# A conditioned transformer layer: the second norm made tile by tile on VectorE with Newton steps, and its rows of blocks 1 to 13 turned on VectorE through DRAM

## The chip, the core and the metric

The kernel runs on one core of a Trainium2 chip. A core has five engines that run their own instruction queues side by side and meet only at semaphores: TensorE (PE in the profile; PEld are its weight loads), VectorE (DVE), ScalarE (ACT), GpSimd (POOL), and SyncE (SP), which here issues the DMA transfers. Matmul results land in PSUM, everything else on the chip lives in SBUF, and weights and activations come from DRAM. The metric is the device time of one execution in microseconds (us).

## What is computed

The reference is one transformer layer whose two norms are shifted, scaled and gated by a condition. Cut to what matters (8 sequences of 1024 tokens, 512 channels, 16 heads, float32):

```python
mod = silu(condition) @ Wada + bada
sh_a, sc_a, gt_a, sh_m, sc_m, gt_m = split(mod, 6, axis=1)
xn = layernorm(x, g1, be1)
xm = xn * (1.0 + sc_a) + sh_a
x = x + gt_a * attention(xm, Wqkv, Wproj, bproj)     # causal, 16 heads of 32
xn = layernorm(x, g2, be2)                            # the second norm
xm = xn * (1.0 + sc_m) + sh_m
h = gelu(xm @ W1 + b1)
x = x + gt_m * (h @ W2 + b2)
```

`layernorm` subtracts the mean of a row and multiplies by `rsqrt(var + 1e-5)`. The two pairs of vectors around a norm (its own gain and bias, and the shift and scale of the condition) are folded into one gain and one shift for each channel.

## The kernel before

**Blocks and steps.** The 8192 tokens are cut into 16 blocks of 512 (`NB`, two to a sequence), a block into four tiles of 128 rows (`NTT`). A window of the plan (`plan[w]`) holds linear steps: for block w-1 the output projection (`proj`), the second norm's modulated rows (`mt`), the feed-forward's up steps (`u`, four) and down steps (`d`, four); for block w+1 the query and key steps (`k`, `q`); for block w the value step (`v`); and for block w+2 the load, the first norm and its modulated rows (`load_xa`, `norm_a`, `at`). Beside these runs the attention of block w (`attend`): scores into a PSUM region of four banks (`st`), their row maxima on VectorE (line 1556), the exponential on ScalarE (line 1644), the sums of the weights on GpSimd (line 1762). The big linear steps are multiplied with Strassen's seven products (`strassen`), so each takes sums of its operands: `modulated` leaves both the modulated rows (`xm`) and their sums (`t`).

**What sets the order.** The kernel is written by a planner that runs when the program is built. It keeps a modelled clock for each engine (`now`), notes each instruction's modelled length (`note`, `note_pe`, `note_act`), and records next the thread (linear main, linear sides, attention) whose operands are ready first. The recorded order of each engine is then fixed: on the chip an engine works through its own list in that order and waits where an operand is late. `note(..., port=True)` lets a VectorE instruction start after the GpSimd instruction that the model has running at that time. Work that has no fixed place stands in lists (`jobs` for VectorE, `act_jobs`, `pool_jobs`) that are emptied when the model has the engine free. `either` puts an addition on VectorE or GpSimd, `sooner` puts an operation on VectorE or ScalarE, by the modelled clocks. Three PSUM banks (`banks`) serve all linear products, eight SBUF slots (`RING`) the weights, which SP fetches in the order of use as slots come free.

**The second norm before.** `project_out(n)` makes the four tiles of the projection: 16 matmul groups, for each tile the product with the gate row (line 193, VectorE) and the addition to the residual `xr` (`add_to`, VectorE or GpSimd). Behind the last tile `normalize` puts four jobs for VectorE in the list (`bn_stats`, `bn_aggr`, lines 590 and 591); the last of them records `power` on GpSimd (lines 612 to 615: add epsilon, power -1/2, two operations for the offset, on 128x4 each), and four applications of the norm (`apply_tile`) on ScalarE (line 631) or VectorE (line 626) into the tile `hat`, of which there is one buffer. `modulated` then turns the rows into columns on TensorE: 16 matmuls against the identity for a block (line 735), four into a bank, and a modulation of each bank by ScalarE (line 745) or VectorE (line 739). `by_pe` names the norms treated so: all second norms (m0 to m15) and the first norms a0 and a1.

**The first norm of blocks 2 to 15** takes the other way already: the same `normalize`, then `turn`: four stream transposes of 32x32 blocks on VectorE (line 671), a DMA of the 1 MB tile to DRAM (`held`, line 680), four DMAs back into the `hat` tile with the pieces in their places (line 685), and modulations from SBUF. The planner allows 8000 ns (`HOLDING`) for each way.

Of the kernel before, what the change touches and what calls it, by code (L numbers as in the profile page):

```python
# [8 lines left out]

F32 = mybir.dt.float32  # L10
BF16 = mybir.dt.bfloat16
AF = mybir.ActivationFunctionType
ALU = mybir.AluOpType
AX = mybir.AxisListType
# [3 lines left out]
EPS = 1e-5  # L18
# [4 lines left out]
def kernel(  # L23
# [204 lines left out]
    def mlp_steps(n):  # L228
# [62 lines left out]
    def pieces_of(step):  # L291
# [112 lines left out]
    minus_half = const.tile([P, NTT], F32, tag="minus_half", name="minus_half")  # L404
    nc.gpsimd.memset(minus_half, -0.5)
# [171 lines left out]

    hats = {}

    def normalize(tiles, key, sources):  # L580

        for t in range(NTT):
            written["hat", key, t] = NEVER
        mv = small.tile([P, NTT, 2], F32, tag="mv", name=f"mv_{key}")
        rstd = small.tile([P, NTT], F32, tag="rstd", name=f"rstd_{key}")
        offset = small.tile([P, NTT], F32, tag="offset", name=f"offset_{key}")

        def statistics(t):
            st = small.tile([P, nc.vector.BN_STATS_DIM], F32, tag="st", name=f"st_{key}_{t}")
            nc.vector.bn_stats(st, tiles[:, t, :])  # L590
            nc.vector.bn_aggr(mv[:, t, :], st)
# [12 lines left out]
        def root():  # L604
            nc.scalar.activation(rstd, mv[:, :, 1], AF.Sqrt, bias=eps)
            note_act(300, "sqrt", [("mv", key)], [("rstd", key)])
            nc.vector.reciprocal(rstd, rstd)
            nc.vector.scalar_tensor_tensor(offset, mv[:, :, 0], -1.0, rstd, ALU.mult, ALU.mult)
            note("DVE", 360, [("rstd", key)], [("rstd", key)], port=True)

        def power():
            nc.gpsimd.tensor_scalar(rstd, mv[:, :, 1], EPS, None, ALU.add)
            nc.gpsimd.tensor_tensor(rstd, rstd, minus_half, ALU.pow)
            nc.gpsimd.tensor_scalar(offset, mv[:, :, 0], -1.0, None, ALU.mult)
            nc.gpsimd.tensor_tensor(offset, offset, rstd, ALU.mult)
            note("POOL", 1500, [("mv", key)], [("rstd", key)])

        to = [None]

        def apply_tile(t):  # L620
            if t == 0:
                hats[key] = to[0] = hat_tile(key) if key[0] == "m" else tiles
            xh, xt = to[0][:, t, :], tiles[:, t, :]
            reads, writes = [("rstd", key)], [("hat", key, t)]
            if (key == "a0" and t % 2) if alone[0] else sooner(reads, writes, 700, 800) == "DVE":
                nc.vector.tensor_scalar(
                    xh, xt, rstd[:, t : t + 1], offset[:, t : t + 1], ALU.mult, ALU.add
                )
                note("DVE", 700, reads, writes, port=True)
            else:  # L630
                nc.scalar.activation(
                    xh, xt, AF.Identity, bias=offset[:, t : t + 1], scale=rstd[:, t : t + 1]
                )
                note_act(800, None, reads, writes)

        for t in range(NTT):
            add_job(lambda t=t: statistics(t), [sources[t]], key[0] == "m")

    def normalize_tile(xt, key, t, source):

# [22 lines left out]
    def turn(key, rows, xm):  # L663

        small_blocks = xm.rearrange("p c n -> p (c n)")
        by_tile = small_blocks.rearrange("p (m h t i) -> p h m t i", m=NTT, h=NC, t=NTT)
        written["blocks", key] = NEVER

        def turn_tile(t):
            into = by_tile[:, :, :, t, :]  # L670
            nc.vector.transpose(into, rows[:, t, :].rearrange("p (h m i) -> p h m i", m=NTT, i=Q))
# [8 lines left out]
        nc.sync.dma_start(held, small_blocks)  # L680
        written["held", key] = now["PE"] + HOLDING
        yield [("held", key)], []
        for m in range(NTT):
            some = held[:, ts(m, D)].rearrange("(a i) d -> i a d", i=Q)
            nc.sync.dma_start(rows[ts(m, Q), :, :], some)
        written["turned", key] = now["PE"] + HOLDING
        yield [("turned", key)], []
# [4 lines left out]
    def modulated(key, gain, shift, b, guards):  # L692
        for t in ("B11", "B21", "B22", "T1", "T2", "T3", "T4"):
            written[key, t] = NEVER
        turned = key not in by_pe
        if turned:
            yield [*(("hat", key, t) for t in range(NTT)), *guards], []
        else:
            yield [("hat", key, 0), *guards], [BANK]
        got = hats.pop(key)  # L700
# [312 lines left out]
    def project_out(n):  # L1013
# [2 lines left out]
        attT = qTs[n]  # L1016
        tiles = [residual[n][:, t, :] for t in range(NTT)]
        last = n == NB - 1
        begun = []

        def begin(t):
# [6 lines left out]
        for t, xt in enumerate(tiles):  # L1028
# [34 lines left out]
    def up(step):  # L1063
        _, n, q = step
# [217 lines left out]
    def perform(step):  # L1282
# [25 lines left out]
        elif kind == "mt":  # L1308
            n = step[1]
            guards = [("v done", n + 1)]  # L1310
            start(modulated(f"m{n}", *columns_of["m"], blocks[n][0], guards))
        elif kind == "k":
            if step[1] != 3:
# [625 lines left out]
```

## Time and profile before

| | |
|---|---|
| Time, median of 3 runs (lowest to highest) | 3546.16 us (3545.45 to 3546.95) |
| Time of the profiled execution | 3542.2 us |
| Its span, first to last instruction | 3540.5 us |
| Granted TensorE clock, mean | 0.998 |
| Busy: PE, DVE, POOL, ACT | 98%, 61%, 59%, 34% |
| Moved by DMA | 465.96 MB, 132 GB/s on average |

A row of a group gives line, engine, operation, tiles and shapes, the count, then the busy time in us and the mean duration of one in ns, then the idle time of the engine just before them and what ended it. A row of a timeline gives the start and the length in us; neighbours of one kind are merged. Float32 matmuls stand in the trace as two instructions each, and four of them, one for each group of 32 columns or rows, run side by side, so the busy time of a group is far below count times mean. A PE that is busy all the time has no idle time to lose; what it does can still be shortened, and idle time can be added.

### The profile page before, as it was taken

The numbers are of one execution on the slowest core, as the hardware profiler recorded it, in microseconds if no ns is written. First come the engines' busy times: TensorE is split into PE (matmuls) and PEld (weight loads), VectorE is DVE, ScalarE is ACT, GpSimd is POOL, SyncE is SP. The second block draws the span as 40 slices with busy tenths as digits, with TensorE's granted clock in tenths as the row PEclk, the third lists the DMA queues.
The fourth block names the chain that finished last, engine by engine and source line by source line (L and its number), as shares of the span: only waits on it lengthen the run. The fifth ranks groups of instructions, "written<-read, shape, count | busy, mean of one in ns | idle before, by whom it ended". The sixth has DMA issues, their size and how long they took to land.

```text
span 3540.5 us, 120499 instructions
## 1 busy us (share of the span) xinstructions
PE 3482.5 (98%) x54621; PEld 1738.0 (49%) x54621; DVE 2174.2 (61%) x2383; ACT 1190.1 (34%) x1237; POOL 2074.9 (59%) x2249
## 2 busy tenths in 40 slices
PE   8999999999999999999999999999999999999999
PEld 4444445445554555545554454544545445454445
DVE  5776675564756557565675656656566556655563
ACT  2334323352333513235232342323423234232521
POOL 2667836666376664666546675366762667526660
PEclk9999999999999999999999999999999999999999
DMA  6753434335443354524445334443344533443334
GB/s 198 245 163 103 137 117 140 111 111 156 117 148 103 110 160 117 168 85 126 142 118 159 103 115 141 124 149 107 118 132 127 156 106 119 135 126 124 100 110 140
DMA packets 319555, 465.96 MB, mean 132 GB/s; under 512 B 26300, under 2 KB 176636, under 8 KB 316996
## 3 DMA queue, kind: packets, MB, share of 16 engines
q1 hardware_dynamic: 318928, 458.22, 42.9%
q8 instruction: 430, 7.05, 0.8%
q14 instruction: 81, 0.66, 0.1%
q10 hardware_dynamic: 116, 0.03, 0.0%
HBM read 412.99 MB, written 43.06 MB: 129 GB/s over the span
## 4 chain that ended last, share of the span: by engine, by line
PE 88%; DMA 4%; DVE 3%; POOL 2%; issue 1%; ACT 1%; SPq 0%; ACTq 0%; DVEq 0%; POOLq 0%
PE bank L202 61%; PE sc L1541 8%; PE po L1672 7%; PE st L1632 7%; PE st L1620 3%; DMA w<-in_L_cond_Wproj_dram 2%; PE bank L1693 2%; PE bank L735 1%; DVE mx L1556 1%; POOL pT L1762 1%; DMA w<-in_L_cond_Wada_dram 1%; PE bank L1594 0%; POOL hT L161 0%; POOL xr L161 0%; DVE sc L1553 0%
## 5 line engine op out<-in xcount | busy, mean ns | idle before, releaser
L1762 POOL TENSOR_TENSOR pT<-pT,pT 128x256 f32<-128x256 f32 (+3 forms) x1254 | 1207.2, 998 | 347.9 <-PE po L1672 181.4
L1644 ACT ACTIVATE pT<-st 128x2048 f32<-128x2048 f32 x288 | 541.0, 1879 | 1000.5 <-PE st L1632 883.3
L202 PE MATMUL bank<-w,hT 128*32 128x256 f32 x14336 | 812.3, 380 | 1.1 <-ACT rec L1702 0.9
L1556 DVE TENSOR_REDUCE mx<-sc 128x4 f32<-128x2048 f32 (+3 forms) x384 | 666.0, 1755 | 197.7 <-PE sc L1541 191.6
L202 PEld LDWEIGHTS bank<-w,hT 128*32 128x32 f32 x14336 | 450.4, 110 | 369.2 <-issue 81.4
L202 PE MATMUL bank<-xm_m,w 128*32 128x256 f32 x8192 | 499.6, 381 | 0.0
L202 PE MATMUL bank<-t_m,w 128*32 128x256 f32 x6144 | 381.2, 380 | 0.0
L1649 POOL TENSOR_SCALAR_AFFINE_SELECT pT<-pT 128x512 f32<-128x512 f32 x256 | 168.8, 677 | 346.6 <-ACT pT L1644 344.2
L202 PEld LDWEIGHTS bank<-xm_m,w 128*32 128x32 f32 x8192 | 255.7, 110 | 224.7 <-issue 62.4
L1553 DVE TENSOR_TENSOR sc<-sc,mask 128x1024 f32<-128x1024 f32 (+1 forms) x160 | 162.9, 1018 | 319.7 <-PE sc L1541 242.5
L1541 PE MATMUL sc<-kT,qT 32*128 32x512 f32 (+3 forms) x3072 | 329.1, 520 | 1.8 <-DVE mx L1556 1.1
L1672 PE MATMUL po<-pT,v 128*32 128x512 f32 (+3 forms) x3048 | 302.9, 492 | 2.0 <-POOL pT L1649 2.0
L1632 PE MATMUL st<-qT,kT 32*128 32x512 f32 (+3 forms) x3072 | 301.0, 487 | 0.0
L202 PEld LDWEIGHTS bank<-t_m,w 128*32 128x32 f32 x6144 | 190.0, 110 | 173.3 <-issue 48.5
L202 PE MATMUL bank<-xm_a,w 128*32 128x256 f32 x3968 | 249.3, 382 | 0.0
L202 PE MATMUL bank<-w,qT 128*32 128x512 f32 x2048 | 238.2, 594 | 8.7 <-DMA w<-in_L_cond_Wproj_dram 7.2
L1711 DVE RECIPROCAL rec<-rec 128x128 f32<-128x128 f32 x256 | 225.7, 920 | 31.5 <-ACT rec L1702 31.5
L1541 PEld LDWEIGHTS sc<-kT,qT 32*128 32x128 f32 x3072 | 129.3, 183 | 179.3 <-issue 73.0
L193 DVE TENSOR_TENSOR hT<-bank,u_u 128x512 f32<-128x512 f32 x192 | 129.9, 687 | 114.1 <-PE bank L202 107.4
L202 PE MATMUL bank<-t_a,w 128*32 128x256 f32 x2944 | 188.4, 382 | 0.4 <-ACT xm_m L745 0.4
L1069 ACT ACTIVATE hT<-hT,cols 128x512 f32<-128x512 f32 x256 | 164.4, 711 | 35.5 <-DVE hT L193 35.0
L202 PEld LDWEIGHTS bank<-xm_a,w 128*32 128x32 f32 x3968 | 122.7, 110 | 105.5 <-issue 32.6
(216 smaller groups left out, 3384.6 us busy)
## 6 DMA issues: line engine op xcount, KB each, us to landing
w<-in_L_cond_W_dram SPq DMA_DIRECT2D x384, 256.0 KB
w<-kept_up_S SPq DMA_DIRECT2D x256, 256.0 KB
w<-kept_down_S SPq DMA_DIRECT2D x256, 256.0 KB
w<-kept_qkv_S SPq DMA_DIRECT2D x180, 256.0 KB
w<-in_L_cond_Wqkv_dram SPq DMA_DIRECT2D x147, 256.0 KB
hat_a<-in_x_dram SPq DMA_DIRECT2D x64, 256.0 KB
xr<-in_x_dram SPq DMA_DIRECT2D x32, 512.0 KB
w<-in_L_cond_Wproj_dram SPq DMA_DIRECT2D x64, 256.0 KB
```

What stands on the lines that cost most here:

```text
L193: nc.vector.tensor_tensor(out, src, other, op)
L202: nc.tensor.matmul(ps[r, :], columns, rhs, start=start, stop=stop, skip_group_check=True)
L1069: nc.scalar.activation(hT[:, i, :], hT[:, i, :], AF.Gelu, bias=cols[:, O_B1 + f : O_B1 + f + 1])
L1541: nc.tensor.matmul(sc[:, j, c0 : c0 + w], qTs[n][r, gg, ts(qt, P)], keys_of(n, kh)[r, gg, :w], start=True, stop=True, skip_group_check=True,)
L1553: nc.vector.tensor_tensor(place, place, shape_of.to_broadcast(place.shape), ALU.add)
L1556: nc.vector.tensor_reduce(maxima[n, gg][:, kh, qt, :], sc[:, :, c0 : c0 + w], axis=AX.X, op=ALU.max)
L1632: nc.tensor.matmul(st[:, j, c0 : c0 + w], kT[r, gg, ts(k % NTT, P)], qT[r, gg, TB - w :], start=False, stop=True, skip_group_check=True,)
L1644: nc.scalar.activation(pT[:, :, :used], st[:, :, :used], AF.Exp, scale=scale)
L1649: nc.gpsimd.affine_select(diagonal, diagonal, pattern=[[0, HPG], [1, P]], compare_op=ALU.is_ge, fill=0.0, base=0, channel_multiplier=-1,)
L1672: nc.tensor.matmul(po[r, TB - w :], v[:, k % NTT, g * P + j * hd : g * P + (j + 1) * hd], pT[:, j, c0 : c0 + w], start=(k == 0), stop=last ...
L1711: nc.vector.reciprocal(some, some)
L1762: nc.gpsimd.tensor_tensor(into, into, pT[:, j, c0 : c0 + w], ALU.add)
```

## The change

The second norm of blocks 0 to 14 no longer waits for the whole projection. Behind each tile of the projection the residual addition goes to VectorE always, and `statistics_at_once` takes that tile's statistics right there; behind the second and the fourth tile it also makes the inverse root and the offset of the two tiles, and puts the two applications in the list. The root is made by `inverse_root` on VectorE: half of variance plus epsilon, a first guess from the bits of the number (a shift and a multiply-add on the integers), and three Newton steps of three instructions; with the offset 13 instructions on 128x2. The first norm of blocks 2 to 15 (`normalize`) uses the same 13 instructions, on 128x4, in place of the four on GpSimd. The rows of the second norm of blocks 1 to 13 are turned by `turn` as those of the first norm are, each tile's stream transpose recorded as soon as its row tile is planned to be ready; blocks 0, 14 and 15 stay with TensorE. `mt` of blocks 1 to 13 is moved ahead of `proj` in the plan, so that it can start while the projection runs. The pending GpSimd additions (`run_pool_jobs`) are recorded ahead of the projection.

```diff
+    by_pe = {"a0", "a1", "m0", f"m{NB - 2}", f"m{NB - 1}"}
...
+    for steps in plan.values():
+        for step in [s for s in steps if s[0] == "mt" and f"m{s[1]}" not in by_pe]:
+            steps.remove(step)
+            steps.insert(steps.index(("proj", step[1])), step)
...
-    by_pe = {f"m{n}" for n in range(NB)} | {"a0", "a1"}
...
+    GUESS = float(0x5F3759DF - (1 << 22)) - 2.0**31
+    def inverse_root(out, variance, key):
+        size = [P, out.shape[1]]
+        half_of = small.tile(size, F32, tag=f"half{size[1]}", name=f"half_{key}")
+        square = small.tile(size, F32, tag=f"square{size[1]}", name=f"square_{key}")
+        nc.vector.tensor_scalar(half_of, variance, EPS, 0.5, ALU.add, ALU.mult)
+        bits = out.bitcast(I32)
+        nc.vector.tensor_scalar(bits, half_of.bitcast(I32), 1, None, ALU.logical_shift_right)
+        nc.vector.tensor_scalar(bits, bits, -1.0, GUESS, ALU.mult, ALU.add)
+        for _ in range(3):
+            nc.vector.tensor_tensor(square, out, out, ALU.mult)
+            nc.vector.tensor_tensor(square, square, half_of, ALU.mult)
+            nc.vector.scalar_tensor_tensor(out, square, 1.5, out, ALU.subtract, ALU.mult)
...
         def power():
-            nc.gpsimd.tensor_scalar(rstd, mv[:, :, 1], EPS, None, ALU.add)
-            nc.gpsimd.tensor_tensor(rstd, rstd, minus_half, ALU.pow)
-            nc.gpsimd.tensor_scalar(offset, mv[:, :, 0], -1.0, None, ALU.mult)
-            nc.gpsimd.tensor_tensor(offset, offset, rstd, ALU.mult)
-            note("POOL", 1500, [("mv", key)], [("rstd", key)])
+            inverse_root(rstd, mv[:, :, 1], key)
+            nc.vector.scalar_tensor_tensor(offset, mv[:, :, 0], -1.0, rstd, ALU.mult, ALU.mult)
+            note("DVE", 1000, [("mv", key)], [("rstd", key)], port=True)
...
+    def statistics_at_once(tiles, key, t, source, kept_of={}):
+        pair = t // 2
...
+        nc.vector.bn_stats(st, tiles[:, t, :])
+        nc.vector.bn_aggr(mv[:, t % 2, :], st)
+        note("DVE", 850, [source], [("mv", key)], port=True)
+        if t % 2 == 0:
+            return
...
+        inverse_root(rstd, mv[:, :, 1], f"{key}_{pair}")
+        nc.vector.scalar_tensor_tensor(offset, mv[:, :, 0], -1.0, rstd, ALU.mult, ALU.mult)
+        note("DVE", 1000, [("mv", key)], [("rstd", key, pair)], port=True)
+        def apply(i):
...
+        for i in (t - 1, t):
+            act_jobs.append((lambda i=i: apply(i), [("rstd", key, pair)]))
...
         for t in range(NTT):
-            add_job(lambda t=t: turn_tile(t), [("hat", key, t)], key[0] == "m")
+            if key[0] == "m":
+                yield [("hat", key, t)], []
+                turn_tile(t)
+            else:
+                add_job(lambda t=t: turn_tile(t), [("hat", key, t)])
...
+        run_pool_jobs(True)
...
             else:
-                add_to(xt, y, [ky], [("xr", n, t)])
+                nc.vector.tensor_tensor(xt, xt, y, ALU.add)
+                note("DVE", 700, [ky, ("xr", n, t)], [("xr", n, t)], port=True)
+                statistics_at_once(residual[n], f"m{n}", t, ("xr", n, t))
...
-        run_pool_jobs(True)
         bias_row(n, "m")
-        if not last:
-            normalize(residual[n], f"m{n}", [("xr", n, t) for t in range(NTT)])
```

More of the change, by code (lines that the diff above doesn't have):

```diff
@@ L11 @@
 BF16 = mybir.dt.bfloat16
+I32 = mybir.dt.int32
 AF = mybir.ActivationFunctionType
@@ L637, in normalize @@
             add_job(lambda t=t: statistics(t), [sources[t]], key[0] == "m")
+    def statistics_at_once(tiles, key, t, source, kept_of={}):
+        pair = t // 2
+        if t % 2 == 0:
+            kept_of[key, pair] = small.tile([P, 2, 2], F32, tag=f"mv{pair}", name=f"mv_{key}_{pair}")
+        mv = kept_of[key, pair]
+        st = small.tile([P, nc.vector.BN_STATS_DIM], F32, tag="st", name=f"st_{key}_{t}")
+        nc.vector.bn_stats(st, tiles[:, t, :])
+        nc.vector.bn_aggr(mv[:, t % 2, :], st)
+        note("DVE", 850, [source], [("mv", key)], port=True)
+        if t % 2 == 0:
+            return
+        rstd = small.tile([P, 2], F32, tag=f"rstd{pair}", name=f"rstd_{key}_{pair}")
+        offset = small.tile([P, 2], F32, tag=f"offset{pair}", name=f"offset_{key}_{pair}")
+        inverse_root(rstd, mv[:, :, 1], f"{key}_{pair}")
+        nc.vector.scalar_tensor_tensor(offset, mv[:, :, 0], -1.0, rstd, ALU.mult, ALU.mult)
+        note("DVE", 1000, [("mv", key)], [("rstd", key, pair)], port=True)
+        def apply(i):
+            if i == 0:
+                kept_of[key] = hats[key] = hat_tile(key)
+            xh, xt = kept_of[key][:, i, :], tiles[:, i, :]
+            by = slice(i % 2, i % 2 + 1)
+            reads, writes = [("rstd", key, pair)], [("hat", key, i)]
+            if sooner(reads, writes, 700, 800) == "DVE":
+                nc.vector.tensor_scalar(xh, xt, rstd[:, by], offset[:, by], ALU.mult, ALU.add)
+                note("DVE", 700, reads, writes, port=True)
+            else:
+                nc.scalar.activation(xh, xt, AF.Identity, bias=offset[:, by], scale=rstd[:, by])
+                note_act(800, None, reads, writes)
+        for i in (t - 1, t):
+            act_jobs.append((lambda i=i: apply(i), [("rstd", key, pair)]))
     def normalize_tile(xt, key, t, source):
@@ L1018, in project_out @@
         last = n == NB - 1
+        run_pool_jobs(True)
+        for t in range(NTT):
+            written["hat", f"m{n}", t] = NEVER
         begun = []
@@ L1310, in perform @@
             guards = [("v done", n + 1)]
+            for t in range(NTT) if f"m{n}" not in by_pe else ():
+                written["hat", f"m{n}", t] = NEVER
             start(modulated(f"m{n}", *columns_of["m"], blocks[n][0], guards))
```

7 lines of the change are left out of this document (4 added, 3 removed).

## The prediction

> **What bounds the kernel now.** I read the page first (busy times, then the chain that ended last), then the windows, the groups by shape, and the timelines of one projection.
>
> ```profile
> PE 3482.5 (98%) x54621; PEld 1738.0 (49%) x54621; DVE 2174.2 (61%) x2383; ACT 1190.1 (34%) x1237; POOL 2074.9 (59%) x2249
> PE 88%; DMA 4%; DVE 3%; POOL 2%; issue 1%; ACT 1%; SPq 0%; ACTq 0%; DVEq 0%; POOLq 0%
> ```
> ```profile
> 1105.00:1326.00 221.00, 220.24 (x3464) 110.08 (x3464) 129.32 (x141) 84.38 (x85) 143.79 (x155) 1.00 0.42 125
> 642.00:656.00 14.00, 14.00 (x136) 4.05 (x132) 8.21 (x7) 2.84 (x3) 7.20 (x10) 1.00 0.17 51
> 656.00:684.00 28.00, 28.00 (x364) 12.24 (x360) 22.81 (x28) 12.74 (x13) 22.00 (x23) 1.00 0.30 89
> ```
>
> TensorE is the bound: 98% busy, 88% of the chain, and in a sixteenth of the span (first window) idle for 0.8 us of 221, at full clock. So only work taken from TensorE, or waits put into it, move the time. The second window is most of a projection, the third the stretch behind it with the second norm: there VectorE is 81% and GpSimd 79% busy. That is where the change adds to VectorE.
>
> **What leaves TensorE.** 13 blocks times 16 transposes are 208 of these 256:
>
> ```profile
> L735 PE MATMUL bank<-ident,hat_m 128*128 128x128 f32 x256 | 46.0, 297 | 3.6 <-ACT hat_m L658 3.6
> ```
> ```profile
> 671.34 0.33 PE L735 MATMUL bank<-ident,hat_m 128*128 128x128 f32 x1
> 671.60 0.64 PE L202 MATMUL bank<-xm_a,w 128*32 128x256 f32 x8
> 672.17 0.33 PE L735 MATMUL bank<-ident,hat_m 128*128 128x128 f32 x1
> ...
> 677.78 1.09 PE L735 MATMUL bank<-ident,hat_m 128*128 128x128 f32 x8
> 678.80 1.07 PE L202 MATMUL bank<-t_a,w 128*32 128x256 f32 x16
> 679.80 0.66 PE L735 MATMUL bank<-ident,hat_m 128*128 128x128 f32 x4
> 680.39 0.85 PE L202 MATMUL bank<-t_a,w 128*32 128x256 f32 x12
> ```
>
> By the group's busy time they hold 46.0 * 208/256 = 37 us. The timeline adds the change of form. A lone transpose delays the next product by 0.26 us (671.34 to 671.60). Of these products 8 last 0.64 us and 32 last 1.90 (a row below), so one more costs 0.053; the 8 behind the lone transpose should take 0.42 us to the next instruction and take 0.57: 0.15 more, together 0.41. The run of 8 takes 1.02 and that of 4 takes 0.59, each with some 0.15 on entering. This block has four lone ones, one run of 8 and one of 4: 1.64 + 1.17 + 0.74 = 3.5 us; without any change of form it would be 37/13 = 2.8. I take 3.25 for a block, **42 us less** in all (ends 37 and 46).
>
> **What VectorE gets.** The listed order of the changed program has 41 more residual additions there, 52 stream transposes, 44 root chains of 13 instructions (30 on 128x2 for the second norms, 14 on 128x4 for the first), and loses 24 modulations from PSUM, 11 applications of the norm and 16 bias additions; GpSimd loses the 41 additions and four operations for each of 29 norms. Prices:
>
> ```profile
> L161 POOL TENSOR_TENSOR xr<-xr,y 128x512 f32<-128x512 f32 x41 | 52.6, 1286 | 112.0 <-DVE y L193 111.9
> L158 DVE TENSOR_TENSOR xr<-xr,y 128x512 f32<-128x512 f32 x19 | 20.2, 1064 | 0.6
> L671 DVE STREAM_TRANSPOSE xm_a<-hat_a 128x512 f32<-128x512 f32 x56 | 34.6, 672 | 0.0
> L739 DVE TENSOR_SCALAR xm_m<-bank,gainm,shiftm 128x512 f32<-128x512 f32 x27 | 21.9, 811 | 30.7 <-PE bank L735 30.7
> L590 DVE BATCH_NORM_STATS2 st_m<-xr 128x6 f32<-128x512 f32 x60 | 40.1, 668 | 0.4 <-POOL xr L161 0.4
> L591 DVE BATCH_NORM_AGGREGATE mv_m<-st_m 128x2 f32<-128x6 f32 x60 | 10.9, 182 | 2.1
> L613 POOL TENSOR_TENSOR rstd_m<-rstd_m,minus_half 128x4 f32<-128x4 f32 x15 | 15.7, 1047 | 1.2
> L1556 DVE TENSOR_REDUCE mx<-sc 128x4 f32<-128x2048 f32 x192 | 439.8, 2291 | 194.4 <-PE sc L1541 191.6
> ```
>
> The additions cost 41 * 1.06 = 43 us, the transposes 52 * 0.67 = 35, the modulations give back 24 * 0.81 = 19. The planner knows their lengths (700 and 620 ns, with the running GpSimd instruction allowed for), so it places them; VectorE has 39% idle to hold them. I cost them at nothing; the cover is that idle time. The relief of GpSimd (53 us of additions, 29 powers of 1.05 us and more) is off the path and gains nothing by itself.
>
> **The root chains** are the step where the plan and the chip part. A small VectorE instruction on two SBUF operands is short alone and long beside GpSimd:
>
> ```profile
> L1570 DVE TENSOR_TENSOR mx<-mx x32: 165/675/1339, 195.8 to 3359.0; 128x16 f32<-128x16 f32 x32
> ```
> ```profile
> 2338.19 1.23 DVE L1575 CAST mcols<-mx 128x16 bf16<-128x16 f32 x1
> 2339.45 1.18 DVE L1576 TENSOR_TENSOR rest<-mx,mcols 128x16 f32<-128x16 f32 x1
> 2340.66 1.23 DVE L1577 CAST mcols<-rest 128x16 bf16<-128x16 f32 x1
> 2341.93 0.23 DVE L1578 TENSOR_TENSOR mcols<-rest,mcols 128x16 bf16<-128x16 f32 x1
> ```
> ```profile
> 2336.84 4.99 POOL L1762 TENSOR_TENSOR pT<-pT,pT 128x512 f32<-128x512 f32 x4
> ```
>
> While GpSimd runs its four additions (to 2341.83), each VectorE instruction ends with one of them; the last, behind them, takes 0.23. So a chain of 13 costs between 13 * (0.17 + 0.04) = 2.7 us (GpSimd idle) and 13 * 1.25 = 16 us (GpSimd never idle); the plan notes 1.0 us. Between these I take 2.7 / (1 - share of GpSimd's own work): during a projection that share is (7.20 - 2 * 1.28 for the additions that leave) / 14 = 0.33, so 4.0 us; for the first norms the span's 0.59, so 6.6 us. VectorE is late by 3.0 and by 5.6 us.
>
> The Trainium skill (SBUF — State Buffer, Who interferes with whom) has the shared port pair as an exclusive lock: the loser waits for the whole instruction, and an instruction with two SBUF inputs competes for it too. The rows agree on VectorE's side (1.18 to 1.23 us beside 1.25 us additions). By that rule alone, with GpSimd always running, a chain would take the 16 us of the upper end, and the sum would be that of the third rival.
>
> How much of a delay reaches TensorE? Two prices:
>
> ```profile
> 642.39 1.14 PE L1541 MATMUL sc<-kT,qT 32*128 32x512 f32 x8
> 643.46 3.64 PE L202 MATMUL bank<-w,qT 128*32 128x512 f32 x32
> ```
> ```profile
> 627.19 1.90 PE L202 MATMUL bank<-w,xm_a 128*32 128x256 f32 x32
> ```
> ```profile
> L1575 DVE CAST mcols<-mx 128x16 bf16<-128x16 f32 x8 | 8.6, 1081 | 0.2
> L1576 DVE TENSOR_TENSOR rest<-mx,mcols 128x16 f32<-128x16 f32 x8 | 11.6, 1450 | 0.3
> L1577 DVE CAST mcols<-rest 128x16 bf16<-128x16 f32 x8 | 10.8, 1354 | 0.5
> L1578 DVE TENSOR_TENSOR mcols<-rest,mcols 128x16 bf16<-128x16 f32 x8 | 3.5, 442 | 0.3
> ```
> ```profile
>   DVE mcols L1578: 4.2, 4
> ```
>
> First, by the changed order: in block 2 the first chain is followed on VectorE by a maximum over scores. TensorE has, from the end of the second tile, those scores (1.1 us) and 56 products (6.2 us) before it needs that region again: 7.3 us. VectorE needs the matmul's tail 0.4, product 0.69, addition 0.69, statistics 0.85, chain 1.0 as planned and maximum 2.29: 5.9. The slack is 1.4 us, and 3.0 us late means 1.6 us of waiting. The second chain has scores and 96 shorter products (5.1 us) ahead: 6.2, slack 0.3, waiting 2.7. That is 4.3 for a block, 65 for fifteen. Second, the eight sequences of the kind shown above are noted as 0.72 us in the plan and take 34.5/8 = 4.3, so they are late by 3.6; TensorE's wait for their results is the 4.2 us of the last row in all, 0.5 each: 13 us for 30 chains late by 3.0. The first is nearer, since a maximum stands directly behind these chains, but it is counted in one block and takes no gap of VectorE in between: I take 2.7 for a block, **40 us**. The first norm's chains are jobs set where the model has VectorE idle: ends 0.5 and 5.6 - 1.4 = 4.2 each, nearer the lower, 1.2: **17 us** (7 to 59).
>
> **The turn through DRAM.** 13 times a DMA of 1 MB out and four back, 5 issues more on SP, ahead of the weights of `k` and `q` that stand behind them there.
>
> ```profile
> 610.60 0.38 SPq L680 DMA_DIRECT2D held_a<-xm_a  x1
> 618.07 2.42 SPq L685 DMA_DIRECT2D hat_a<-held_a  x4
> ```
> ```profile
> 627.83 1.52 ACT L745 ACTIVATE xm_a<-hat_a,shifta,gaina 128x512 f32<-128x512 f32 x2 [3.26 <-DMA hat_a<-held_a]
> ```
> ```profile
>   ACT xm_a L745: 45.5, 11
>   DVE xm_a L739: 22.0, 12
> ```
>
> A first norm's turn takes 7.5 us out (610.60 to 618.07) and 9.8 back, against 8.0 planned each way. With the chain (4.0), two applications, transposes and modulations (3 + 1.3 + 1.6) and the steps before it (2.6), rows are ready some 30 us behind the projection. In the changed order TensorE has, by the two rows of products above, about 33 us of `k`, `q` and attention before the first `u` product in blocks 2 to 13, 27 in block 1. So `u` does not wait in most blocks; the cover is those two steps, and without it each block would pay up to 30 us. What does wait is ScalarE and VectorE in their queues (45.5 and 22.0 us for 14 turns, exponentials behind them). TensorE pays between 0 and 13 * 4.1 = 53 us; beside its 0.8 us of idle in a whole window I take 5. SP's issues (2.8 us for a block) lie in a stretch with DMA at 0.17 to 0.30.
>
> **Sum.** -42 + 40 + 17 + 5 = +20 us on the span of 3540.5, so 3560 for the span and 3562 for the profiled execution's 3542.2. The median of the runs lies 4 us above that: **3566**.
>
> **Rivals.** (1) The waits of the chains are small, as after the eight sequences: 13 + 7 + 2 us against 42, so -20, 3526: faster. It decides once all added waits stay under 42 us, just under 1 us for each of 44 chains. For it speaks that VectorE's long instructions beside GpSimd cost TensorE almost nothing now (0.8 us idle in 221); against it, that a chain is late by several us at once, directly before a maximum. (2) The turn is the late part: `u` waits some 4 us more in each of 13 blocks because the 9.8 us landing and the late chain add up, or SP holds the weights back: 20 + 50, 3616. For it: 33 us against 30 is little room. Against it: once TensorE has waited for a chain, the turn has that time too. (3) GpSimd is busy through the chains: with 10 us for a chain, half of the 9 us reaching TensorE, 44 * 4.5 = 198 against 57 in the sum: 3707. Against it: once TensorE waits, no new exponentials come, and GpSimd runs dry. (4) Gain and waits cancel, within 7 us of 3546.
>
> Beside rival 2: the Trainium skill (VectorE: DVE Perf Modes, Rules for kernel authors) says to transpose 128x128 on TensorE where PSUM will do, since VectorE turns 32x32 blocks only; no run here has compared the two yet.
>
> **How the numbers follow.** Forecast (3553 to 3590) 0.39; rival 1 0.33, rival 2 0.12, rival 3 0.06, rival 4 0.10. A measurement here tells 0.2%, 7 us, from no change. So slower 0.57, same 0.10, faster 0.33. The range reaches to rival 1 with the larger gain and no wait for DMA, 3512, and past rival 2 to 3640; the rest of rival 3 and the low tail of rival 1 stay out, under 2 in 10. The likeliest case and the slower rivals alone would be 3553 to 3690.
>
> **What would show it.** Right: 48 transposes left on line 735, TensorE's busy time down by some 40 us and its idle time up by some 60; the chain's small instructions at 0.2 us and at 1.2 us mixed, VectorE's busy time up by 200 us or more; TensorE waiting on line 1618 (the maxima in the new numbering). Wrong: TensorE's idle time unchanged and the span 20 to 40 us shorter (rival 1); its waits on the modulations or on weights (rival 2). Chains of 2.7 us throughout would make the forecast wrong on the faster side, of 10 us on the other.

## The result, and the profile after

The changed kernel takes 3639.4 us (median of 4 runs, 3638.1 to 3642.8) against 3545.8 beside it: a ratio of 1.0266, 95% interval 1.0248 to 1.0284. It is slower by 94 us. The forecast was 3566: the sign was right, the size too small by 73 us.

The busy line of the page after, and the span with the mean granted clock:

```profile
PE 3492.8 (96%) x54413; PEld 1735.7 (48%) x54413; DVE 2357.2 (65%) x3017; ACT 1216.4 (33%) x1273; POOL 1972.1 (54%) x2091
```
```profile
core 0: 3636.2 us, clock 0.985
```

TensorE's idle time went from 3540.5 - 3482.5 = 58.0 to 3636.2 - 3492.8 = 143.4 us: 85 more. The clock says the rest: at a mean of 0.985 the span holds 0.015 * 3636 = 54.5 us of missing clock, before 0.002 * 3540 = 7.1, so 47 more. Not all of that is time: where TensorE is idle anyway, a slow clock costs nothing. By the clock record of the two traces TensorE is busy for 92 us at half clock after and for 12 before; half of that, 46 and 6 us, is the price of the slower matmuls, 40 more. TensorE's busy time rose by 10 although 208 transposes left; with the slow clock taken out, it fell by 29. So -29 + 40 + 85 is the 96 us between the two spans. About a third of what was added is not waiting but slower matmuls.

The window that was the quiet one before (0.8 us idle, clock 1.00) now has 9.5 us of idle. Columns: length, then the busy time of PE, PEld, DVE, ACT and POOL, the clock, the DMA share, GB/s:

```profile
1105.00:1326.00 221.00, 211.52 (x3208) 101.20 (x3202) 145.26 (x184) 83.46 (x83) 129.56 (x136) 0.99 0.43 126
```

What TensorE and ScalarE waited for, after (us in total, times, longest), and the row of before that answers to the second:

```profile
ACT hat_m L685 <- DVE offset_m L672: 131.5, 28, 22.3
...
PE st L1682 <- DVE mx L1618: 54.5, 26, 6.5
...
PE bank L203 <- ACT p_u L189: 11.3, 5, 3.9
...
PE bank L203 <- DVE xm_m L797: 1.5, 1, 1.5
```
```profile
PE st L1620 <- DVE mx L1556: 7.4, 6, 2.4
```

TensorE now waits for the row maxima, 47 us more than before, and hardly at all for the modulated rows that come back from DRAM. The third row is a wait for a bank drain: ScalarE (line 189) or VectorE (line 194) copies a finished product out of its PSUM bank before the bank can be used again. The groups of the new work:

```profile
L793 PE MATMUL bank<-ident,hat_m 128*128 128x128 f32 x48 | 9.8, 342 | 6.2 <-ACT hat_m L710 3.3 <-ACT hat_m L685 2.9
...
L1115 DVE TENSOR_TENSOR xr<-xr,y 128x512 f32<-128x512 f32 x60 | 48.6, 809 | 3.8
L596 DVE TENSOR_TENSOR square_m<-rstd_m 128x2 f32<-128x2 f32 x90 | 22.1, 246 | 3.1
L597 DVE TENSOR_TENSOR square_m<-square_m,half_m 128x2 f32<-128x2 f32 x90 | 21.5, 239 | 3.1
L598 DVE SCALAR_TENSOR_TENSOR rstd_m<-square_m,rstd_m 128x2 f32<-128x2 f32 x90 | 18.5, 205 | 3.1
L596 DVE TENSOR_TENSOR square_a<-rstd_a 128x4 f32<-128x4 f32 x42 | 18.1, 431 | 1.4
```

One chain with what it does to TensorE (timeline, start and length in us):

```profile
488.57 8.70 POOL L1824 TENSOR_TENSOR pT<-pT,pT 128x256 f32<-128x256 f32 x12
...
490.96 3.21 PE L203 MATMUL bank<-xm_a,w 128*32 128x256 f32 x56
...
492.82 0.93 DVE L597 TENSOR_TENSOR square_m<-square_m,half_m 128x2 f32<-128x2 f32 x1
493.78 0.92 DVE L598 SCALAR_TENSOR_TENSOR rstd_m<-square_m,rstd_m 128x2 f32<-128x2 f32 x1
494.73 0.92 DVE L596 TENSOR_TENSOR square_m<-rstd_m 128x2 f32<-128x2 f32 x1
495.68 0.38 DVE L597 TENSOR_TENSOR square_m<-square_m,half_m 128x2 f32<-128x2 f32 x1
...
497.33 0.16 DVE L598 SCALAR_TENSOR_TENSOR rstd_m<-square_m,rstd_m 128x2 f32<-128x2 f32 x1
497.52 0.16 DVE L672 SCALAR_TENSOR_TENSOR offset_m<-mv_m,rstd_m 128x2 f32<-128x2 f32 x1
497.60 0.70 DVE L1615 TENSOR_TENSOR sc<-sc,mask 128x512 f32<-128x512 f32 x1
498.34 2.29 DVE L1618 TENSOR_REDUCE mx<-sc 128x4 f32<-128x2048 f32 x1
500.68 0.61 PE L1682 MATMUL st<-mrow,minus_ones 32*128 32x512 bf16 x4 [6.51 <-DVE mx L1618]
```

The chain runs from 490.1 to 497.7 us, one instruction for each of GpSimd's additions (the trace has them in widths of 256, 384 and 128; the row merges them under the first), and at 0.16 us only when these have ended at 497.3. The mask and the maximum stand behind it on VectorE, and TensorE waits 6.5 us for the maximum. Now the clock of the same stretch:

```profile
490.80:494.20 3.40, 3.37 (x64) 1.77 (x56) 3.26 (x5) 0.00 (x0) 3.40 (x5) 1.00 0.55 156
494.20:497.60 3.40, 0.00 (x0) 0.00 (x0) 3.16 (x8) 0.00 (x0) 3.07 (x6) 1.00 0.19 66
497.60:501.00 3.40, 0.32 (x4) 0.32 (x8) 3.37 (x4) 1.99 (x3) 0.00 (x0) 0.50 0.00 0
501.00:504.40 3.40, 3.40 (x24) 0.92 (x20) 3.40 (x6) 1.24 (x1) 0.00 (x0) 0.50 0.37 154
504.40:507.80 3.40, 3.40 (x64) 1.60 (x58) 2.54 (x4) 0.64 (x1) 1.92 (x2) 1.00 0.68 236
```

Behind 3.4 us without a matmul the clock is at 0.50 for 6.8 us, also in the 3.4 us in which TensorE is busy again from end to end. The Trainium skill (TensorE: Matmul & The Clock Gate, What's actually happening) describes this gate: half the clock after an idle window of about 3.4 us, the full one after as long a busy one. By this row the trace agrees; shorter waits are looked at further down.

Not every chain is like this one. How long a chain takes goes with what GpSimd does beside it. Here are a chain of a second norm with GpSimd silent and a chain of a first norm with GpSimd busy throughout (columns as above):

```profile
693.68:696.21 2.53, 2.53 (x56) 1.50 (x50) 2.08 (x14) 0.59 (x1) 0.00 (x0) 1.00 0.60 159
1238.68:1247.10 8.42, 7.29 (x121) 3.71 (x120) 7.97 (x14) 1.88 (x1) 8.42 (x14) 1.00 0.21 66
```

Of the 44 chains, 19 take 2.53 to 2.6 us, and 18 take 4 to 8.6 us. From its start to 5 us behind its end, a chain of 4 us or more has 3.3 us of TensorE idle time beside it on average, a shorter one 0.6. Beside all 44 there are 75 us of it, and the 18 long ones (7 of the second norms', 11 of the first norms') hold 60.

### The profile page after: what moved, and what is told of

Same layout as the page of the kernel before. It is cut to its first block, busy times and chain, and to the rows that moved or that the text cites. A ratio compares the mean times of both kernels' runs of the same rounds, so it can differ in the third digit from the quotient of the medians.

```text
span 3636.2 us, 120801 instructions
## 1 busy us (share of the span) xinstructions
PE 3492.8 (96%) x54413; PEld 1735.7 (48%) x54413; DVE 2357.2 (65%) x3017; ACT 1216.4 (33%) x1273; POOL 1972.1 (54%) x2091
## 5 line engine op out<-in xcount | busy, mean ns | idle before, releaser
L203 PE MATMUL bank<-xm_m,w 128*32 128x256 f32 x8192 | 505.0, 385 | 12.8 <-ACT p_u L189 11.3
L1694 PE MATMUL st<-qT,kT 32*128 32x512 f32 (+3 forms) x3072 | 310.7, 498 | 0.0
L1798 POOL TENSOR_TENSOR qT<-top,rec 128x512 f32<-128x512 f32 x61 | 81.3, 1332 | 209.0 <-DVE rec L1773 198.5
```

The source lines that it names most:

```text
L203: nc.tensor.matmul(ps[r, :], columns, rhs, start=start, stop=stop, skip_group_check=True)
L1694: nc.tensor.matmul(st[:, j, c0 : c0 + w], kT[r, gg, ts(k % NTT, P)], qT[r, gg, TB - w :], start=False, stop=True, skip_group_check=True,)
L1798: nc.gpsimd.tensor_tensor(qTs[n][:, g, :], top, rec, ALU.mult)
```

## The experiments

Theory: the 44 root chains on VectorE hold up the maxima and the bank drains that stand behind them, and the rest of the change is about neutral. The rivals: the turn through DRAM is late, or the early statistics disturb the plan. "Over e1" below is against 3540.8 us.

### e1, e2, e3: the roots back on GpSimd

All 44 (e1), the 14 of the first norms (e2) or the 30 of the second (e3); all else as changed:

```diff
-        inverse_root(rstd, mv[:, :, 1], f"{key}_{pair}")
-        nc.vector.scalar_tensor_tensor(offset, mv[:, :, 0], -1.0, rstd, ALU.mult, ALU.mult)
+        nc.gpsimd.tensor_scalar(rstd, mv[:, :, 1], EPS, None, ALU.add)
+        nc.gpsimd.tensor_tensor(rstd, rstd, minus_half[:, :2], ALU.pow)
+        nc.gpsimd.tensor_scalar(offset, mv[:, :, 0], -1.0, None, ALU.mult)
+        nc.gpsimd.tensor_tensor(offset, offset, rstd, ALU.mult)
```

> The changed kernel with all 44 inverse roots back on GpSimd (four operations with a power, noted 1500 ns, for each pair of tiles and for each first norm); the turn through DRAM, the statistics tile by tile and the additions on VectorE stay. Theory (the 13-instruction chains on VectorE make TensorE wait, and each long wait brings a stretch at half clock): the 73 us of TensorE idle time around the chains and most of the 48 us of added clock loss go, 3639 - 73 - 40 = about 3525, below the kernel before; TensorE idle 60 to 75 us, clock 0.995 or more. Rival (the turn through DRAM and the additions moved to VectorE cause the waits): 3600 or more.

> The changed kernel with only the 14 roots of the first norm back on GpSimd. Theory: the 36 us of idle time at these chains and the 20 us of clock loss behind them go, about 3583, and together with the next run the two differences add up to that of the run with all roots on GpSimd. Rival: 3630 or more.

> The changed kernel with only the 30 roots of the second norm back on GpSimd. Theory: 38 us of idle time and 15 us of clock loss go, about 3586. Rival: 3630 or more.

e1: 3540.8 us, ratio 0.9991 (0.9982 to 1.0001). e2: 3585.7, 1.0116 (1.0100 to 1.0131). e3: 3575.6, 1.0090 (1.0073 to 1.0107). The waits and the clock of e1:

```profile
PE st L1688 <- DVE mx L1624: 11.8, 11, 2.6
```
```profile
core 0: 3545.2 us, clock 0.993
```

The chains cost 99 us, the whole loss and a little more. e1 is 16 us over its theory all the same; e5, e8 and e6 show where that went. That figure holds the chains and what the planner writes differently when the roots are GpSimd's; e10 and e13 below keep the order. Taken out alone, the first norms' 14 are worth 54 and the second norms' 30 are worth 64, more than 99 together. Put into e1 alone they cost 35 (e3 over e1) and 45 (e2 over e1), less than 99 together. So each kind costs more where the other is there too, and the 99 has no one split. The forecast had 17 and 40.

### e9: the chains on VectorE, but for nothing

e1 with each chain still issued, into a tile that nobody reads:

```diff
+        inverse_root(spare, mv[:, :, 1], f"{key}_{pair}")
+        nc.vector.scalar_tensor_tensor(spare, mv[:, :, 0], -1.0, spare, ALU.mult, ALU.mult)
```

> The changed kernel with its 44 inverse roots on GpSimd again (as in e1, 3540.8 us), but each of the 44 chains of Newton steps still issued on VectorE, into a spare tile that nobody reads. Theory A, VectorE's occupied time is the price, since the maxima, the additions and the drains of the banks stand behind the chain on its in-order queue: nearly the whole 99 us of e1 comes back, 3615 us or more, with TensorE idle 120 us or more. Rival B, the late root is the price (rows are normalised, turned and multiplied later): the chains are harmless here, 3560 us or less, and idle stays near the 74 of e1.

3604.3 us, ratio 1.0172 (1.0157 to 1.0187): 64 over e1.

```profile
ACT hat_m L699 <- POOL offset_m L682: 65.7, 13, 20.0
...
PE st L1696 <- DVE mx L1632: 54.3, 30, 4.7
...
PE bank L203 <- ACT p_u L189: 1.5, 2, 0.8
```

TensorE's wait for the maxima is back in full (the second row, 54.3 against 54.5 us), though no row waits for these chains. So two thirds of the price are VectorE's time, as the theory has it; the figure is under theory A's 3615 all the same. The other 35 us come only where the root is also needed. The waits show half of them: the normalisation stands in ScalarE's queue and waits there for the offset, 131.5 us in the changed kernel and 65.7 here, and TensorE's waits for ScalarE, all rows together, are 38 us there, 20 here and 19 in e1. That fits a late root which also holds up what stands behind the normalisation on ScalarE, the drains (third row, 1.5 us here and 11.3 there) and the exponentials. The rest of the 35 us stays open; the planner's order differs between these runs too.

### e10 and e13: shorter and longer chains

One Newton step instead of three (7 instructions instead of 13, with a coarser root), or five (19). The planner's 1000 ns stay, so the recorded order is that of the changed kernel: in the three traces all other instructions of VectorE, GpSimd and ScalarE follow each other in the same order.

```diff
-        for _ in range(3):
+        for _ in range(1):     # e13: range(5)
```

> The changed kernel with one Newton step instead of three, so 7 instructions a chain instead of 13 (the root is then good to about 0.2% only: two steps are left out). Theory A, the price goes by the length of the chain: 7/13 of the 99 us that the chains cost, 3594 us. Rival B, the price grows faster than the length, since a wait below some 2 us leaves the granted clock alone: 3580 us or less, with under 20 us lost to half clock beyond the 26 of e1. Rival C, a price per chain whatever its length: 3620 us or more.

> The changed kernel with five Newton steps instead of three, 19 instructions a chain instead of 13. Over e1 (roots on GpSimd) 7 instructions cost 27 us and 13 cost 99. Theory A, the price goes by length above a threshold of some 5 instructions (about 12 us for each further one): 3541 + 171 = 3712 us, with 100 us or more lost to half clock. Rival B, it goes in proportion to length (99/13 = 7.6 us for each instruction): 3541 + 145 = 3685 us. Rival C, it flattens, since a longer chain only makes the same waits longer and the planner's other work fills in: 3665 us or less.

e10: 3567.4 us, ratio 1.0064 (1.0049 to 1.0079). e13: 3717.9, 1.0493 (1.0478 to 1.0507). e10 comes out under its rival B's 3580, e13 near its theory A's 3712. Their waits for the maxima, and the clocks (e10, then e13):

```profile
PE st L1682 <- DVE mx L1618: 21.2, 20, 3.5
```
```profile
core 0: 3558.8 us, clock 0.994
```
```profile
PE st L1682 <- DVE mx L1618: 77.0, 28, 7.7
```
```profile
core 0: 3716.7 us, clock 0.975
```

| instructions in a chain | 0 (e1) | 7 (e10) | 13 (changed) | 19 (e13) |
|---|---|---|---|---|
| median over e1, us | 0 | 27 | 99 | 177 |
| mean length of a chain, second / first norm, us | | 1.9 / 3.1 | 3.5 / 5.7 | 4.7 / 7.6 |
| TensorE idle from a chain's start to 5 us behind its end, all second / all first, us | | 13 / 12 | 39 / 36 | 73 / 56 |
| half of TensorE's busy time in half-clock stretches that begin from a chain's start to 8 us behind its end, second / first, us | | 3 / 2 | 12 / 18 | 30 / 25 |

The lengths are means over the chains of each trace, the two rows below them are sums. Idle and clock together make 30, 105 and 184 us, close to the medians (a little more, since some of these waits are there without a chain). From 7 to 13 and from 13 to 19 instructions nothing but the length differs, and over all 44 chains each instruction costs 12 to 13 us. The first seven cost 3.8 us each over e1, whose order is another. The price is not in proportion: short chains disappear in slack, and little clock is lost behind them. An instruction from the 8th on costs three times what one of the first seven does.

How long a wait has to be can be counted. Over all seventeen traces of this case, between 221 and 3400 us of the span, the idle gaps of TensorE over 0.1 us that begin at full clock, and how many have a half-clock stretch beginning in them or within 4.5 us of their end:

| gap, us | under 1.5 | 1.5 to 2.0 | 2.0 to 2.6 | 2.6 to 3.0 | over 3.0 |
|---|---|---|---|---|---|
| gaps | 699 | 60 | 52 | 21 | 82 |
| followed by half clock | 15 | 3 | 41 | 17 | 79 |

The step lies at 2 us. The Trainium skill (TensorE: Matmul & The Clock Gate, Why this matters for your kernels) warns of gaps above about 3 us; here four in five of the gaps between 2.0 and 2.6 us were already followed by half clock, and the measurement decides.

### e4: the chains alone, in the kernel before

```diff
-            nc.gpsimd.tensor_tensor(rstd, rstd, minus_half, ALU.pow)
+            inverse_root(rstd, mv[:, :, 1], key)
```

(with the other three lines of `power`, for 29 norms)

> The kernel before with one thing changed: the 29 roots outside the start and the last block (14 of the first norm, 15 of the second, each on 128x4) by the 13 instructions on VectorE in place of four on GpSimd; transposes stay on TensorE. Theory: each costs what a first norm's chain costs in the changed kernel, 2.5 us of idle time and 1.5 us of clock, 29 * 4 = 116, about 3660; at the least half of it, 3600. Rival (the turn and the additions are the cause): 3546 to 3560.

3712.0 us, ratio 1.0473 (1.0457 to 1.0488).

```profile
PE bank L750 <- ACT hat_m L646: 76.8, 12, 7.1
```

In the old order 29 chains cost 169 us, more than 44 in the new, and more than the 116 forecast: there TensorE makes the transposes itself and waits 76.8 us for the normalised rows. The turn is not what makes the difference: without it, but with early statistics, 44 chains cost 88 us (e6 over e8, below). Early statistics take the norm out of TensorE's way; they do not take the chain out of VectorE's.

### e5, e8, e6: the turn and the early statistics, one without the other

e5 is the kernel before with only the turn of blocks 1 to 13 through DRAM (the new `by_pe`, the old `normalize`). e8 is e1 without the turn: statistics at once and additions on VectorE, roots on GpSimd, all second norms turned on TensorE. e6 is the changed kernel without the turn.

```diff
-    by_pe = {f"m{n}" for n in range(NB)} | {"a0", "a1"}
+    by_pe = {"a0", "a1", "m0", f"m{NB - 2}", f"m{NB - 1}"}     # e5; reversed in e8 and e6
```

> The kernel before with one thing changed: the rows of the second norm of blocks 1 to 13 are turned on VectorE and through DRAM (the steps keep their places, the statistics stay in the list behind the projection, the roots on GpSimd). Theory: the turn gives the 42 us of transposes and costs at most 10 in waits for DMA, 3543 - 35 = about 3508. Rival (the turn eats its own gain, by late rows or by SP): 3535 or more, with waits for DMA in front of the modulations.

> The kernel before with the statistics tile by tile and the additions on VectorE alone: roots on GpSimd, transposes on TensorE. It tells where the 42 us went that the run with all roots on GpSimd did not gain. If the additions and statistics in line cost nothing, 3543, and the turn gives nothing by itself; if they cost what the turn gives, 3575 to 3585.

> The changed kernel with all second norms' transposes on TensorE again; the chains, the statistics tile by tile and the additions on VectorE stay. Theory (the chains are the loss, the turn a gain): 3639 + 35 to 42 = about 3678. Rival (the turn is part of the loss): below 3635.

e5: 3587.8 us, ratio 1.0128 (1.0112 to 1.0143), a miss for the theory: 208 transposes fewer, and 44 us slower. e8: 3567.5, 1.0067 (1.0050 to 1.0084). e6: 3655.8, 1.0313 (1.0298 to 1.0329), between its theory and its rival. So the early statistics alone cost 24 us, the turn alone costs 44, and both (e1) cost nothing: the turn gains 27 on e8 and 16 on e6. Block 1 of e5, timeline:

```profile
483.98 1.29 DVE L671 STREAM_TRANSPOSE xm_m<-hat_m 128x512 f32<-128x512 f32 x2
485.30 0.34 SPq L680 DMA_DIRECT2D held_m<-xm_m  x1
487.50 1.70 PE L1541 MATMUL sc<-kT,qT 32*128 32x512 f32 x8 [3.13 <-DVE mx L1556]
489.19 1.75 SPq L685 DMA_DIRECT2D hat_m<-held_m  x4
491.59 0.62 PE L1620 MATMUL st<-mrow,minus_ones 32*128 32x512 bf16 x4 [2.39 <-DVE mx L1556]
496.94 2.93 ACT L745 ACTIVATE xm_m<-hat_m,shiftm,gainm 128x512 f32<-128x512 f32 x4
500.14 0.69 PE L1511 MATMUL bank<-kT,qT 32*128 32x512 f32 x1 [2.16 <-DVE mx L1528]
502.44 1.08 PE L202 MATMUL bank<-xm_m,w 128*32 128x256 f32 x8
```

From the last stream transpose (485.3) to the first modulation (496.9) the rows are away. TensorE has only attention left and waits for one maximum after another; the waits carry the names of the maxima, but what is missing is the linear work in between. Over the 13 blocks the rows are away for the same 17 us on average in e5, e1 and the changed kernel, and TensorE is idle in these stretches for 35 us in all in e5, and for 3 us in e1 and in the changed kernel, all of it in block 1. So what the early statistics and the earlier place in the plan buy is other work to put beside the turn; which of the two does it was not separated. What they cost shows in e8, in waits that are not in the list of the kernel before at all:

```profile
PE bank L203 <- ACT p_q L189: 4.5, 6, 0.8
PE bank L203 <- ACT qT L189: 4.2, 6, 0.7
...
PE bank L203 <- ACT kT L189: 2.4, 6, 0.4
PE bank L203 <- DVE kT L194: 2.4, 6, 0.4
```

These are drains of the banks of `q` and `k`, 13.5 us of the 16 us of idle that e8 has more than the kernel before (3565.4 - 3491.5 = 73.9 against 58.0). Why the drains come late there and not in e1 was not tried.

### e7: the planner told the true lengths

```diff
-        note("DVE", 1000, [("mv", key)], [("rstd", key, pair)], port=True)
+        note("DVE", 3500, [("mv", key)], [("rstd", key, pair)], port=True)     # 5700 for the first norm
```

> The changed kernel, same instructions, with the planner told what a chain takes in the trace: 3500 ns for a pair of the second norm, 5700 for a first norm, in place of 1000. Theory A (the loss is the plan being late, since TensorE's order counts on 1.0 us): TensorE idle falls by half or more, 3580 or less. Theory B (VectorE has no room for chains of that length between the maxima, however they are planned): within 15 us of 3639.

3605.7 us, ratio 1.0169 (1.0154 to 1.0185), 34 less than the changed kernel and between the two theories. The planner can hide a third of the price if it knows it. In the profiled execution the gain is as much clock as waiting: slower matmuls cost 22 us there in place of 46, idle time is 122 in place of 143. Why the rest stays was not tried.

### e11, e12, e14, e15: what is left when the chains are gone

All four start from e1. e11 lets the planner place the residual additions again; e12 turns block 1 on TensorE; e14 does both; e15 adds block 13.

```diff
-                nc.vector.tensor_tensor(xt, xt, y, ALU.add)
-                note("DVE", 700, [ky, ("xr", n, t)], [("xr", n, t)], port=True)
+                add_to(xt, y, [ky], [("xr", n, t)])
...
-    by_pe = {"a0", "a1", "m0", f"m{NB - 2}", f"m{NB - 1}"}
+    by_pe = {"a0", "a1", "m0", "m1", f"m{NB - 3}", f"m{NB - 2}", f"m{NB - 1}"}     # e15
```

> e1 (changed kernel, roots on GpSimd) with the 60 residual additions behind the projection placed on VectorE or GpSimd by the planner again, as before the change. Theory A, the additions on VectorE are a part of the 24 us that the early statistics cost in e8: 3530 us or less. Rival B, on GpSimd the addition takes 1.29 us instead of 0.77 and the statistics wait for it, so rows come later: 3541 to 3560 us.

> e1 with block 1 (the first one turned through DRAM) turned on TensorE again, so 12 blocks by DRAM. In e1 the stretch around 487 to 512 us, where block 1's rows come back from DRAM, has two half-clock stretches of 6.8 us and TensorE idle. Theory A, the turn itself costs there, because block 0's MLP is the only work that could fill the gap: 3 us more for 16 transposes, 10 less for the clock, 3 less idle, 3531 us. Rival B, the stall belongs to the attention of the first blocks and stays: 3543 us or more.

> e11 and e12 together: roots on GpSimd, the residual additions placed by the planner, block 1 turned on TensorE. Theory A, the two gains (3 and 7 us below e1's 3541) lie in different stretches and add: 3531 us, 0.34% under the kernel before. Rival B, they are the same stall around 490 to 510 us, so only the larger counts: 3534 to 3537 us.

> e14 with block 13, the last one turned through DRAM, on TensorE too, so 11 blocks by DRAM. In e12 TensorE waits 5.4 us at 3181 us, where the last turned rows are due, and the clock is at half for 10.2 us behind it. Theory A, that wait is for the turned rows: 3 us more for 16 transposes, 5 less idle, 5 less for the clock, 3524 us. Rival B, it belongs to the attention of the last blocks: 3533 us or more.

e11: 3538.1 us, ratio 0.9986 (0.9976 to 0.9995). e12: 3534.2, 0.9973 (0.9964 to 0.9983). e14: 3531.0, 0.9965 (0.9953 to 0.9977). e15: 3529.8, 0.9965 (0.9952 to 0.9977). The additions are worth some 3 us, not resolved from e1. Block 1 is worth 7: it held all the idle time that e1 has beside its turns, and in e12 the half-clock stretches that e1 has at 495 and 505 us are gone. The likely reason is that its rows come back when there is no earlier feed-forward work to fill the gap. Together (e14) they are 10 us under e1, as much as the two add up to. Block 13 gives nothing that can be told in the time, though the half-clock stretch of 10.2 us that e14 has at 3174 us is gone in e15. So the turn and the early statistics, without the chains, beat the kernel before by 0.35% in e14 and e15. The quiet window in e15 is as quiet as it was, with 220.7 of 221 us busy:

```profile
1105.00:1326.00 221.00, 220.72 (x3476) 108.70 (x3472) 140.49 (x155) 82.65 (x83) 150.46 (x162) 1.00 0.44 130
```

## Why the prediction was right in its sign and wrong in its size

The forecast's sum was -42 + 40 + 17 + 5 = +20. Put together from the runs, the parts are +24 (e8), -27 (e1 against e8) and +99 (changed against e1), +96 for the measured +94. (The split goes by the order in which the parts are added: the turn alone costs 44.) So three terms were off, all in the same direction:

- **The root chains, 57 forecast, 99 measured: the step that failed most.** The mechanism was right: instructions of 0.2 us and of longer steps mixed, a chain of 4.0 us forecast for the second norm and 3.5 measured, 6.6 and 5.7 for the first; the wait on line 1618 was named. That TensorE's idle time behind the second norms' chains came out at 39 us for 40 forecast is in part luck: the forecast had a wait in every block, and the trace has 24 us behind 7 long chains and 15 behind the other 23. Two things were missing. The sentence "VectorE is late by 3.0 and by 5.6 us", carried on to the sum, priced waiting as idle time alone. Many waits of 2 us and more brought half clock with them: slower matmuls for 30 us behind chains, 40 in all. And the first norms' 14 chains were put near the lower end, 1.2 us each, because the planner sets them where its model has VectorE idle. The traces show 36 us of idle behind them, 2.5 each; the planner cut a hole of 1.0 us for a chain of 5.7. The evidence for the clock lay in the trace of before, which has such a stretch at 222 us, behind a gap of 2.4 us; the Trainium skill's rule on idle gaps (TensorE: Matmul & The Clock Gate, Why this matters for your kernels) was not weighed.
- **The early statistics and the moved additions, 0 forecast, 24 measured (e8).** "I cost them at nothing; the cover is that idle time" took VectorE's idle share of 39% for room. Whatever room there was, the planner wrote another order around this work, and waits for bank drains came in; why the drains are late stays open.
- **The transposes and the turn, -42 + 5 forecast, -27 measured (e1 over e8).** The 42 was too much, and so was its lower end of 37: with the half clock taken out, TensorE's busy time fell by 29 us from before to after, by 28 in e5, by 30 from e6 to the changed kernel and by 35 from e8 to e1. The delays read beside single transposes, which raised the 37 to 42, did not show in these sums. The wait for the rows, 5 forecast, was indeed small (the modulated rows hold TensorE for 1.5 us by the row above, and 3 us of idle lie beside all 13 turns). Block 1 took 7 us of what is left (e12).

The rivals. Rival 1 (small waits) needed all waits under 42 us, and idle time rose by 85. Even with 7 instructions a chain, where it rose by 38, e10 stands 24 us over the kernel before: the transposes gave less than 42, and the half clock took its part. Rival 2 (the turn late) did not happen here, with 1.5 us of waiting; its mechanism is real, and e5 is it: the same turn with late statistics leaves TensorE 35 us idle while the rows are away. Rival 3 (chains of 10 us) was wrong in mechanism: the longest chain took 8.6 us, the means are 3.5 and 5.7. Rival 4 did not happen.

What the prediction said would show: 48 transposes on the transposing line, yes. TensorE's busy time down by 40: no, up by 10, as half clock stretched the matmuls; this was the sign to look at first. Idle up by 60: up by 85. VectorE's busy time up by 200 or more: 183.

## What to carry to other kernels

Count a chain of tiny dependent instructions on VectorE by what GpSimd does beside it, since it advanced one instruction for each GpSimd addition here, and count as late everything that stands behind it on that queue. Look at the chains one by one and not at their mean: a few long ones made most of the waiting. A power on GpSimd (0.75 us on 128x2 in e1) was the cheaper root, as no row maximum stands behind it. Price a stall of a busy TensorE with a step in it: here, under about 2 us it cost itself, above that up to 1.7 or 3.4 us more (half of a half-clock stretch of 3.4 or 6.8 us, as far as TensorE is busy in it). A transfer that takes rows away is free only where other linear work lies beside it, so move what makes the rows earlier first, and leave a first block that has no such work as it was.

## What the runs showed of the hardware

Half clock came behind gaps of 2.0 to 2.6 us in 41 of 52 cases, and behind gaps under 2 us in 18 of 759; it comes in stretches of 3.4, 6.8 or 10.2 us. In the changed kernel they cost 46 us of slower matmuls, 6 in the kernel before. Eight products of line 1694 took 1.92 us at half clock (at 501.08 us); the same eight, line 1632 in the kernel before, took 1.03 at full clock (at 647.26 us).

The chain at 490 us kept in step with GpSimd: its instructions began 0.95 us apart beside wider additions and 0.41 apart beside narrow ones (494.73 to 495.68, and 495.68 to 496.09, where the next begins), against 0.16 us of their own. With GpSimd silent a chain of 13 took 2.53 us, with GpSimd busy up to 8.6. GpSimd paid nothing that can be seen: beside the chain its additions of 128x384 took 0.99 to 1.00 us, and the median of all 250 in the trace is 1.01. The Trainium skill (SBUF — State Buffer, Who interferes with whom) says that the loser of the shared ports blocks for the whole instruction of the other. VectorE's side agrees, with 0.92 us beside these additions; but the blocking did not last until GpSimd fell silent, as the two alternated, so the chain advanced by one instruction for each addition.
